# Four edits around softplus in a selective-scan kernel: where delta u is formed, how 1 - (1 + e) is added, which side steps stand beside the sums, when rows of B are fetched

## The chip, the core and the metric

The program runs on one core of a Trainium2 chip. Its time is the time of one execution on the device, in microseconds (us); of several runs the median is taken. Lower is better.

## The reference, cut to what matters

Four layers follow each other on an input of 8 images of 48 x 48 positions and 96 channels. Each layer normalises its input in groups of three channels, runs a two-dimensional selective scan on it, and adds the result to its input. The scan walks the 2,304 positions of an image in four orders (row by row and column by column, each forward and backward; K = 4), for 192 inner channels with 16 states each. Layers 0 to 2 have this form:

```python
xz = x @ in_proj_w.T
xpart, z = jnp.split(xz, 2, axis=-1)
xc = silu(depthwise_3x3(xpart) + conv_b)
xs = jnp.stack([x_hw, x_wh, x_hw[..., ::-1], x_wh[..., ::-1]], axis=1)   # four orders
x_dbl = jnp.einsum('bkdl,kcd->bkcl', xs, x_proj_w)
dts, Bs, Cs = jnp.split(x_dbl, [R, R + N], axis=2)
delta = jax.nn.softplus(jnp.einsum('bkrl,kdr->bkdl', dts, dt_proj_w) + dt_proj_b)
def step(h, inp):
    u_t, d_t, b_t, c_t = inp
    h = jnp.exp(d_t[..., None] * A) * h + (d_t * u_t)[..., None] * b_t[:, :, None, :]
    return h, jnp.einsum('bkdn,bkn->bkd', h, c_t)
```

The four outputs are turned back and added, with a skip term D u, then normalised over the channels, multiplied by silu(z) and projected back to 96 channels. Layer 3 computes the same scan by cumulative sums with a small term in a denominator; the kernel does it on the ends of the sequences alone and has a second run of the full sequences behind a condition at its end, which the profiled execution doesn't take.

What the change touches is delta = softplus(v) and the product delta u, which the scan reads as the factor of B.

## The kernel before, in words

**Tiling.** Work goes pair by pair of images (four pairs per layer). The 192 channels of two images make three tiles of 128 partitions: channels 0 to 127 of each image, and the last 64 of both together. For one pair there are 12 groups (tile t, phase ph for rows or columns, direction d), each of three chunks of 768 positions, each chunk of 16 units. A unit n carries two states: the 128 partitions hold 64 channels of state n // 2 and the same 64 channels of state n // 2 + 8, and n % 2 says which half of the channels it is. So layers 0 to 2 have 3 x 4 x 36 = 432 chunks and 6,912 units.

**One unit.** B is wanted as one row spread over 64 partitions, multiplied by delta u; da = exp(delta A); then comes the scan h = da h + b, then h C, then the sum over states.

- Units 2, 5, 7, 10, 13 and 15 are *pooled*: B comes by DMA in spread form (`bb`), POOL multiplies it by delta u (`weigh`, L741), ACT writes the exponential into a PSUM buffer named `b` (L764), DVE scans (L798).
- The other ten take B from rows in SBUF (`brow`) that PE spreads into the PSUM buffer `b` by a bf16 matmul (`spread_rows`, L667); DVE multiplies it by delta u (L794) and scans (L798); the exponential goes to SBUF (`da`, L764).
- In both, POOL multiplies h by the spread row of C (`cb`, L807), and PE adds the products of the states up in the PSUM buffer `acc` (`add_up`, L854), two units later. The two `b` buffers are shared by all units in turn, so unit n can fill its one only after the scan of unit n - 2.

**Softplus.** The generator `prepare` makes delta and delta u for one chunk while the 16 units of the chunk before it run; each `yield` is one step, and one step is taken per unit. A chunk has two halves of 384 positions. For a half: PE forms v (L603); ACT forms e = exp(-|v|), relu(v), then log(1 + e), w1 = 1 + e and w1 = 1 - w1 (L611 to L617); PE adds e + (1 - (1 + e)) + log(1 + e) + relu(v) into one PSUM bank by identity matmuls, in two steps (L623), where e + (1 - (1 + e)) is what the rounding of 1 + e lost; ACT copies the sum four times to SBUF, so that each half of the channels stands on both halves of the partitions (`to_twins`, L578, tile `dl`); DVE multiplies the bank by u in place (`times_u`, L631 for ph 0, L634 for ph 1); ACT copies that four times as well (L578, tile `du`). In layer 3 (class `Edge`, 192 positions) there is one copy and one product.

**Side steps.** The next pair's prologue (convolution, projections) and the last pair's epilogue (normalisation, gate, output projection) are generators too. In `beside`, one side step is taken per unit, none in unit 2; a step is for example one convolution matmul (L312), or an evacuation on ACT.

**Order.** Between two marks the kernel keeps every engine's instructions in the order in which the loop over units issues them. In unit n: the loads of units ahead (`load_b` 5 ahead, `load` 4 ahead), the spread of unit n + 1, the exponential of unit n + 3, the small carry copies on ACT (L682), the product and scan of unit n, the sum of unit n - 2, and `beside`. All DMAs go through SP's queue; the rows of B of a chunk (`brow`, two DMAs, L749) are issued together with the first `cb` of that chunk, in unit 12 of the chunk before.

Of the kernel before, what the change touches and what calls it, by code (L numbers as in the profile page):

```python
# [103 lines left out]
def ss2d_layers_kernel(ctx: ExitStack, tc: tile.TileContext, x_in, consts, weights, out):  # L104
# [55 lines left out]
    nc.vector.tensor_copy(pick, sel[: 2 * NR])  # L160


    twin = cpool.tile([P, 64], F32, name="twin")
    nc.vector.tensor_add(twin, ident[:, 0:64], ident[:, 64:P])

# [14 lines left out]
    nc.vector.tensor_add(centre, ident, off)  # L180
    centre_22 = cpool.tile([P, P], F32, name="centre_22")
    nc.vector.tensor_add(centre_22, ident, off_22)
    minus_group = cpool.tile([DM, DM], F32, name="minus_group")
    nc.scalar.activation(minus_group, group_w, AF.Copy, scale=-1.0)

# [96 lines left out]

    GATED, READY = "gated", "ready"

    def prologue(l, p, short=False, first=False):
        ly = layers[l]
# [282 lines left out]
                state[c.l, c.p]["xd"][c.ph, b, c.d * r : (c.d + 1) * r, c.c0 : c.c0 + c.m],  # L571
            )

    def to_twins(z, at, v):

        for g in range(2):
            for h in range(2):
                nc.scalar.copy(z[64 * h : 64 * h + 64, g, at], v[64 * g : 64 * g + 64])  # L578

    def prepare(c):  # L580
        l, p, t, ph, d = c.l, c.p, c.t, c.ph, c.d
        ly, s = layers[l], state[l, p]
# [10 lines left out]
        for z in range(0, c.m, HALF):  # L593
            m = min(HALF, c.m - z)
            at = slice(z, z + m)

            ps = bank()
            v = ps[:, :m]
            for b in c.batches:
                q0 = 32 * b if t == 2 else 0  # L600
                o = ps[64 * b : 64 * b + 64] if t == 2 else ps
                chans = slice(P, DIN) if t == 2 else slice(0, P)
                nc.tensor.matmul(  # L603
                    o[:, :m], ly.dtw[q0 : q0 + r, k, chans], dts[q0 : q0 + r, at],
                    start=True, stop=True,
                )
# [10 lines left out]
            nc.scalar.activation(w1, w1, AF.Identity, bias=ones, scale=-1.0)  # L617
            yield
            v = bank()[:, :m]
            for i, z1 in enumerate((e, w1, lg, x)):  # L620
                for g in range(2):
                    half = slice(64 * g, 64 * g + 64)
                    nc.tensor.matmul(  # L623
                        v[half], ident[:, half], z1, start=(i == 0), stop=(i == 3)
                    )
                if i % 2 == 1:
                    yield

            def times_u(o):
                if ph == 0:  # L630
                    nc.vector.tensor_mul(o, v, u[:, c.c0 + z : c.c0 + z + m])  # L631
                    return
                r0 = (c.c0 + z) // H
                nc.vector.tensor_mul(  # L634
                    o.rearrange("p (w h) -> p w h", h=H),
                    v.rearrange("p (w h) -> p w h", h=H),
                    u[:, r0 : r0 + m // H, :],
                )

            if isinstance(c, Edge):  # L640
                nc.scalar.copy(c.dl[0], v)
                times_u(c.du[0])
                c.sum_up()
                c.ready = True
                yield
                return

            to_twins(dl, at, v)
            if z + m == c.m:
                if l == NLAYER - 1:  # L650
                    c.sum_up()
                c.ready = True
                yield
            times_u(v)
            yield
            to_twins(du, at, v)
            yield


    def pieces(m):  # L660
# [23 lines left out]
    class Chunk:  # L684
# [52 lines left out]
        def weigh(self, n):  # L737

            if self.pooled(n):
                b = self.b[n][:, : self.m]  # L740
                nc.gpsimd.tensor_mul(b, b, self.du[n % 2])  # L741

        def load(self, n):

            s, m, at = state[self.l, self.p], self.m, slice(self.c0, self.c0 + self.m)
            if n == 0:
                self.brow = rpool.tile([2 * NR, SCAN], BF16, name="brow", tag="brow")
                for j, b in enumerate(range(2) if self.t == 2 else (self.t, self.t)):
                    nc.sync.dma_start(  # L749
                        self.brow[NR * j : NR * j + NR, :m],  # L750
                        s["xb"][self.ph, b, :, self.d, :, at],
                    )
            self.cb[n] = cb = cbpool.tile([P, SCAN], F32, name="cb", tag="cb")
            self.fetch(cb, NS, n)

# [414 lines left out]
    def run(pairs, short):  # L1170
# [58 lines left out]
        for k, ((l, p, unit), c, n) in enumerate(todo):  # L1229
# [172 lines left out]
```

## Time and profile before

| what | value |
|---|---|
| median of 3 runs | 20507.62 us (20500.42 to 20517.71) |
| the profiled execution: its time / its span | 20509.65 us / 20507.7 us |
| busy: POOL, DVE, PE, ACT | 17768.2, 17656.0, 17283.2, 16243.7 us |
| mean granted clock of TensorE | 0.904 |
| DMA, mean over the span | 205 GB/s |
| layers 0 to 2 (scans of L798), first and last | 205 us to 18,562 us |

In the profile a line of a group gives the source line, engine, operation, tiles, shapes and count, then the busy time in us and the mean of one instruction in ns, then the idle time of the engine just before these instructions and what ended most of it. A busy PE is not a PE at its peak, since matmuls are pipelined and their ends are modelled. An fp32 matmul appears as two records.

### The profile page before, as it was taken

The numbers are of one execution on the slowest core, as the hardware profiler recorded it, in microseconds if no ns is written. First come the engines' busy times: TensorE is split into PE (matmuls) and PEld (weight loads), VectorE is DVE, ScalarE is ACT, GpSimd is POOL, SyncE is SP. The second block draws the span as 40 slices with busy tenths as digits, with TensorE's granted clock in tenths as the row PEclk, the third lists the DMA queues.
The fourth block names the chain that finished last, engine by engine and source line by source line (L and its number), as shares of the span: only waits on it lengthen the run. The fifth ranks groups of instructions, "written<-read, shape, count | busy, mean of one in ns | idle before, by whom it ended". The sixth has DMA issues, their size and how long they took to land. (4 is left out here: it accounts for less than half of the span.)

```text
span 20507.7 us, 304889 instructions
## 1 busy us (share of the span) xinstructions
PE 17283.2 (84%) x88322; PEld 7546.6 (37%) x88322; DVE 17656.0 (86%) x14161; ACT 16243.7 (79%) x30020; POOL 17768.2 (87%) x10121
## 2 busy tenths in 40 slices
PE   8888888888888888888888888888888888888886
PEld 2323333333333333333333333333333333335565
DVE  5999999999999999999999999989989989995543
ACT  5777887887887887887877887877877877877776
POOL 5999999999999999999999999999999999995432
PEclk8998998998998999998998999988988998999997
DMA  5888888888888888888888888888888888883221
GB/s 147 223 221 222 219 220 224 222 219 221 220 225 222 219 229 221 221 229 219 221 228 220 217 225 219 218 218 220 217 219 219 220 219 222 219 220 109 76 72 51
DMA packets 1963444, 4200.13 MB, mean 205 GB/s; under 512 B 369456, under 2 KB 720048, under 8 KB 1948592
## 3 DMA queue, kind: packets, MB, share of 16 engines
q1 hardware_dynamic: 1961776, 4180.52, 77.8%
q8 instruction: 726, 11.89, 0.3%
q14 instruction: 942, 7.72, 0.2%
HBM read 4026.64 MB, written 152.27 MB: 204 GB/s over the span
## 5 line engine op out<-in xcount | busy, mean ns | idle before, releaser
L807 POOL TENSOR_TENSOR cb<-cb,da 128x768 f32<-128x768 f32 x4320 | 7831.3, 1817 | 799.5 <-issue 258.3
L854 PE MATMUL acc<-cb,twin 128*64 128x384 f32 x27648 | 7018.1, 542 | 663.6 <-POOL cb L807 660.3
L798 DVE TENSOR_TENSOR_SCAN da<-da,carry,b 128x768 f32<-128x768 f32 x2880 | 5223.3, 1814 | 176.4 <-ACT b L764 2.3
L741 POOL TENSOR_TENSOR bb<-bb,du 128x768 f32<-128x768 f32 x2592 | 4714.0, 1819 | 361.0 <-DMA bb<-xd 207.8
L794 DVE TENSOR_TENSOR b<-du,b 128x768 f32<-128x768 f32 x4320 | 4087.6, 946 | 883.9 <-PE b L667 785.4
L807 POOL TENSOR_TENSOR cb<-cb,bb 128x768 f32<-128x768 f32 x2592 | 4705.1, 1815 | 155.0 <-DVE bb L798 57.1
L667 PE MATMUL b<-brow,pick 96*64 96x512 bf16 (+2 forms) x18816 | 2761.6, 355 | 1787.6 <-DVE da L798 1408.4
L764 ACT ACTIVATE da<-dl,a 128x768 f32<-128x768 f32 x4320 | 4013.6, 931 | 245.8 <-POOL cb L807 214.0
L854 PEld LDWEIGHTS acc<-cb,twin 128*64 128x64 f32 x27648 | 2268.9, 150 | 3089.4 <-issue 1400.3
L798 DVE TENSOR_TENSOR_SCAN bb<-b,carry,bb 128x768 f32<-128x768 f32 x1728 | 3109.0, 1799 | 114.8 <-ACT b L764 53.5
L764 ACT ACTIVATE b<-dl,a 128x768 f32<-128x768 f32 x2592 | 2334.4, 901 | 590.2 <-DVE da L798 558.4
L798 DVE TENSOR_TENSOR_SCAN da<-da,b 128x768 f32<-128x768 f32 x1440 | 2525.4, 1754 | 85.6 <-DVE b L794 0.9
L667 PEld LDWEIGHTS <-pick 96*64 96x64 bf16 x18816 | 974.1, 114 | 4192.1 <-DVE da L798 2506.3
L578 ACT COPY dl<-ps 64x384 f32<-64x384 f32 x3456 | 1635.3, 473 | 756.7 <-PE ps L623 720.7
L312 PE MATMUL ps<-pad,diag 128*128 128x480 f32 (+1 forms) x4320 | 2165.7, 599 | 11.5 <-DVE eyc L1087 9.9
L623 PE MATMUL ps<-du,cst 128*64 128x384 f32 (+1 forms) x7296 | 1709.7, 516 | 93.1 <-ACT du L617 77.0
L578 ACT COPY du<-ps 64x384 f32<-64x384 f32 x3456 | 1635.7, 473 | 190.0 <-DVE ps L634 91.2
L798 DVE TENSOR_TENSOR_SCAN bb<-b,bb 128x768 f32<-128x768 f32 x864 | 1502.2, 1739 | 94.9 <-ACT b L764 40.5
L623 PE MATMUL ps<-dl,cst 128*64 128x384 f32 (+1 forms) x7296 | 1412.4, 483 | 0.0
L312 PEld LDWEIGHTS ps<-pad,diag 128*128 128x128 f32 x4320 | 687.5, 191 | 1211.4 <-issue 1090.1
L603 PE MATMUL ps<-dts,w 6*128 6x384 f32 (+5 forms) x2432 | 946.3, 595 | 176.1 <-DMA dts<-xd 103.7
L611 ACT ACTIVATE du<-ps,w 128x384 f32<-128x384 f32 (+1 forms) x912 | 521.4, 572 | 622.3 <-PE ps L603 611.5
(144 smaller groups left out, 19159.8 us busy)
## 6 DMA issues: line engine op xcount, KB each, us to landing
cb<-xd SPq DMA_DIRECT2D x13952, 192.0 KB
bb<-xd SPq DMA_DIRECT2D x5184, 192.0 KB
brow<-xb SPq DMA_DIRECT2D x864, 72.0 KB
yd<-y SPq DMA_DIRECT2D x48, 1152.0 KB
ey<-yd SPq DMA_DIRECT2D x256, 216.0 KB
cb<-xd SPq DMA_DIRECT2D x128, 384.0 KB
ex<-xs SPq DMA_DIRECT2D x256, 108.0 KB
xd<-xt SPq DMA_DIRECT2D x32, 684.0 KB
```

Source lines behind the costliest of these rows:

```text
L312: nc.tensor.matmul(ps[:, :m], ly.diag[:, int(t == 2), j, :], pad[:, r0 + dy : r0 + dy + nr, dx : dx + W], start=(j == 0), stop=(j == 8),)
L578: nc.scalar.copy(z[64 * h : 64 * h + 64, g, at], v[64 * g : 64 * g + 64])
L603: nc.tensor.matmul(o[:, :m], ly.dtw[q0 : q0 + r, k, chans], dts[q0 : q0 + r, at], start=True, stop=True,)
L611: nc.scalar.activation(e, v, AF.Abs, bias=bias)
L623: nc.tensor.matmul(v[half], ident[:, half], z1, start=(i == 0), stop=(i == 3))
L667: nc.tensor.matmul(o[64 * h : 64 * h + 64], pick[:, b, n : n + 1].to_broadcast([2 * NR, 64]), rows, start=True, stop=True,)
L741: nc.gpsimd.tensor_mul(b, b, self.du[n % 2])
L764: nc.scalar.activation(da, self.dl[n % 2], AF.Exp, scale=layers[self.l].a2[:, int(self.t == 2), n % 2, k, i : i + 1],)
L794: nc.vector.tensor_mul(b, self.du[n % 2], b)
L798: nc.vector.tensor_tensor_scan(way(h), way(da), way(b), start, ALU.mult, ALU.add)
L807: nc.gpsimd.tensor_mul(c, c, h)
L854: nc.tensor.matmul(self.acc[64 * g : 64 * g + 64, a, : self.m // 2], twin, c[:, a, :], start=False, stop=(pair + 2 == NS and not self.turns),)
```

## The change

1. **Delta u ahead of delta's copies, in SBUF.** `times_u` now writes `du[:, 0]` in SBUF and not the PSUM bank, and stands one step ahead of the four copies of delta. The twins of delta u are made by three copies from SBUF to SBUF, since the first of them is where DVE put it.
2. **1 - (1 + e) by a constant row.** ACT's second operation on w1 goes. PE starts each bank with a row of ones (two bf16 matmuls of `unit` with `unit_row`), subtracts w1 by a negated identity `less`, and then adds e, log and relu. The negated identity takes the place of a constant in `cst` that is not read later.
3. **Side steps.** The two steps of each half that issue sums yield `HEAVY`, and `beside` takes no side step there; in units 4, 12 and 14 it takes two.
4. **Rows of B.** `load_rows` issues a chunk's two `brow` DMAs in unit 6 of the chunk before it, in the same pair.

With the changed yields a chunk's steps fall otherwise on the units: the second half's sums on units 10 and 11 (9 and 10 before), its copies of delta on the top of unit 13 (unit 11 before), its copies of delta u on the end of unit 13 as before; the first half's sums stay on units 2 and 3, its copies of delta move from unit 4 to 5 and those of delta u from 5 to 6; the product with u stays on units 4 and 12.

```diff
+    less = cst[:, P : 2 * P]
+    unit = cpool.tile([P, 64], BF16, name="unit")
+    nc.gpsimd.memset(unit, 0.0)
+    nc.gpsimd.memset(unit[0:1], 1.0)
+    unit_row = cpool.tile([P, 1], BF16, name="unit_row")
+    nc.gpsimd.memset(unit_row, 1.0)
...
+    nc.scalar.activation(less, ident, AF.Copy, scale=-1.0)
...
             nc.scalar.activation(w1, e, AF.Identity, bias=ones)
-            nc.scalar.activation(w1, w1, AF.Identity, bias=ones, scale=-1.0)
             yield
             v = bank()[:, :m]
-            for i, z1 in enumerate((e, w1, lg, x)):
+            for g in range(2):
+                nc.tensor.matmul(
+                    v[64 * g : 64 * g + 64], unit, unit_row.to_broadcast([P, m]),
+                    start=True, stop=False,
+                )
+            for w, z1 in ((less, w1), (ident, e), (ident, lg), (ident, x)):
                 for g in range(2):
                     half = slice(64 * g, 64 * g + 64)
-                    nc.tensor.matmul(
-                        v[half], ident[:, half], z1, start=(i == 0), stop=(i == 3)
-                    )
-                if i % 2 == 1:
-                    yield
+                    nc.tensor.matmul(v[half], w[:, half], z1, start=False, stop=(z1 is x))
+                if z1 is e or z1 is x:
+                    yield HEAVY
...
-            to_twins(dl, at, v)
+            times_u(du[:, 0, at])
+            yield
+            for g in range(2):
+                for h in range(2):
+                    nc.scalar.copy(dl[64 * h : 64 * h + 64, g, at], v[64 * g : 64 * g + 64])
             if z + m == c.m:
                 if l == NLAYER - 1:
                     c.sum_up()
                 c.ready = True
+            yield
+            for h in (1, 0):
+                nc.scalar.copy(du[64 * h : 64 * h + 64, 1, at], du[64:P, 0, at])
+            nc.scalar.copy(du[64:P, 0, at], du[0:64, 0, at])
+            if z + m < c.m:
                 yield
-            times_u(v)
-            yield
-            to_twins(du, at, v)
-            yield
...
+            if n == 6 and coming_to < len(chunks):
+                z = chunks[coming_to]
+                if (z.l, z.p) == (l, p):
+                    z.load_rows()
...
             def beside():
-                step(coming)
-
-                for _ in range(10 if l in short else 0 if ends else 1):
+                got = next(coming, None)
+                some = 0 if ends or got is HEAVY else 2 if n in (4, 12, 14) else 1
+                for _ in range(10 if l in short else some):
                     side_step(rest) or side_step(behind, ahead)
```

`load_rows` holds the two `brow` DMAs that stood in `load`; `load` of a chunk's unit 0 calls it, and it does nothing where the rows are there already.

More of the change, by code (lines that the diff above doesn't have):

```diff
@@ L281, in ss2d_layers_kernel @@
     place = {"tiles": 3}
-    GATED, READY = "gated", "ready"
+    GATED, READY, HEAVY = "gated", "ready", "heavy"
     def prologue(l, p, short=False, first=False):
@@ L572, in load_dt @@
             )
[L574 to L578, printed above, removed]
     def prepare(c):
@@ L741, in weigh, with load_rows @@
                 nc.gpsimd.tensor_mul(b, b, self.du[n % 2])
+        def load_rows(self):
+            if self.brow is not None:
+                return
+            self.brow = rpool.tile([2 * NR, SCAN], BF16, name="brow", tag="brow")
+            for j, b in enumerate(range(2) if self.t == 2 else (self.t, self.t)):
+                nc.sync.dma_start(
+                    self.brow[NR * j : NR * j + NR, : self.m],
+                    state[self.l, self.p]["xb"][
+                        self.ph, b, :, self.d, :, self.c0 : self.c0 + self.m
+                    ],
+                )
         def load(self, n):
-            s, m, at = state[self.l, self.p], self.m, slice(self.c0, self.c0 + self.m)
             if n == 0:
[L747 to L752, printed above, removed]
+                self.load_rows()
             self.cb[n] = cb = cbpool.tile([P, SCAN], F32, name="cb", tag="cb")
```

## The prediction

> **What bounds the kernel now.** I read the busy times first, then the stretch of layers 0 to 2 alone, the groups by form, the waits, and a stretch of the timeline. The page's first part, and one window without the start and without layer 3:
>
> ```profile
> PE 17283.2 (84%) x88322; PEld 7546.6 (37%) x88322; DVE 17656.0 (86%) x14161; ACT 16243.7 (79%) x30020; POOL 17768.2 (87%) x10121
> ...
> 300.00:18560.00 18260.00, 15474.38 (x77729) 6322.09 (x77730) 16678.49 (x12545) 14660.40 (x27083) 16969.05 (x9632) 0.91 0.85 221
> ```
>
> In the window (its columns: us; busy PE, PEld, DVE, ACT, POOL; clock, DMA share, GB/s) POOL is busy 93% and DVE 91%. 432 chunks take 18,357 us (205 to 18,562), 42.5 us each; DVE works about 38.9 of them and POOL about 40. So no engine is full; what is lost is lost in waits between two nearly full engines. The groups by form (columns as in section 5 of the page):
>
> ```profile
> L807 POOL TENSOR_TENSOR cb<-cb,da 128x768 f32<-128x768 f32 x4320 | 7831.3, 1817 | 799.5 <-issue 258.3 <-DVE da L798 140.6 <-PE acc L854 66.0
> ...
> L741 POOL TENSOR_TENSOR bb<-bb,du 128x768 f32<-128x768 f32 x2592 | 4714.0, 1819 | 361.0 <-DMA bb<-xd 207.8 <-DMA cb<-xd 55.0 <-DVE da L798 25.5
> L807 POOL TENSOR_TENSOR cb<-cb,bb 128x768 f32<-128x768 f32 x2592 | 4705.1, 1815 | 155.0 <-DVE bb L798 57.1 <-issue 26.1 <-DMA cb<-xd 18.0
> L794 DVE TENSOR_TENSOR b<-du,b 128x768 f32<-128x768 f32 x4320 | 4087.6, 946 | 883.9 <-PE b L667 785.4 <-PE acc L854 89.7 <-PE ps L413 1.5
> ...
> L578 ACT COPY du<-ps 64x384 f32<-64x384 f32 x3456 | 1635.7, 473 | 190.0 <-DVE ps L634 91.2 <-DVE ps L631 52.8
> L578 ACT COPY dl<-ps 64x384 f32<-64x384 f32 x3456 | 1635.3, 473 | 756.7 <-PE ps L623 720.7
> ...
> L617 ACT ACTIVATE du<-du,ones 128x384 f32<-128x384 f32 x864 | 531.7, 615 | 28.2
> ...
> L634 DVE TENSOR_TENSOR ps<-ps,u 128x384 f32<-128x384 f32 x432 | 352.2, 815 | 126.0 <-ACT dl L578 116.3
> ...
> L631 DVE TENSOR_TENSOR ps<-ps,u 128x384 f32<-128x384 f32 x432 | 239.2, 554 | 207.7 <-ACT dl L578 196.3
> ```
>
> POOL loses 799.5 + 361.0 + 155.0 = 1,315.5 us, all that a change could win here. DVE loses 883.9 us before its products with B, almost all to PE's spread rows, and about 201 us (of 312.6; the rest is one wait of 104 us at the start and others outside the window) before the products with u, which wait for the copies of delta. Taking the 4,320 products of L794 in order, ten to a chunk, the idle time falls on units 0, 1 and 11 (83.7, 237.9, 304.2 us); the other seven have 258 together. Why unit 11, the timeline shows:
>
> ```profile
> 6085.33 0.54 PE L854 MATMUL acc<-cb,twin 128*64 128x384 f32 x1 [1.64 <-POOL cb L807]
> ...
> 6085.71 1.77 PE L623 MATMUL ps<-du,cst 128*64 128x384 f32 x7
> ...
> 6087.41 1.04 PE L465 MATMUL ps<-u,w 64*96 64x480 f32 x2
> ...
> 6088.38 0.52 PE L667 MATMUL b<-brow,pick 96*64 96x512 bf16 x4
> ...
> 6088.94 0.96 DVE L794 TENSOR_TENSOR b<-du,b 128x768 f32<-128x768 f32 x1 [1.49 <-PE b L667]
> ```
>
> PE's sum of an earlier unit waits for POOL, and then the softplus sums (1.77 us) and a side step (1.04 us, with about 0.6 us of issue ahead of it) stand before the spread rows of unit 11. Unit 10 is pooled, so DVE has only a scan to do meanwhile, and stalls.
>
> [...] L631 and L634 waited for L578. [...] PE waited 178.9 us in 50 places for rows of B here.
>
> **The change part by part**, per chunk (two halves) and times 432.
>
> *Spread rows of unit 11.* The sums now stand after them. I keep 35 us of the 304 (units 8 and 9 have 27 and 24): 269 us won. The next to stand behind sums are units 4 and 12. Unit 4 has it already, with 9 us of idle in all; unit 12 follows an unpooled unit and has 62.
>
> *Products with u.* They need PE's sums only, which ended a unit before. Their idle of 201 us goes: 190 won. Writing SBUF costs nothing: layer 3's products already do, 355 ns for 192 elements, which is on the same slope as 554 ns for 384.
>
> *Rows of B and the chunk's turn.* Units 0 and 1 lose 322 us, some of it the 178.9 us of rows. The two SP issues (about 0.75 us each) move from unit 12 to 6, past six units of `cb` and `bb` loads; they wait only for an older DMA, the buffer is long free. They get out of the way of the next chunk's first `cb` and `bb`. I take 190 us won; bounds 90 and 320.
>
> *ACT's operation and copies.* L617 goes: 864 x 0.615 = 532 us. Copies of delta u: 3,456 x 0.473 = 1,636 us become 2,592; [...] ACT works 0.85 ms less, but is busy 80% in the window, so this alone is worth nothing on the path; nor is the 720.7 us that it no longer waits for sums.
>
> *Constant rows.* 1,824 bf16 matmuls; a spread of 2 x 512 + 2 x 256 columns takes 0.52 us, so a pair of 384 some 0.25 us: 0.23 ms on PE, ahead of the spread of units 4 and 12. Those end 1.0 and 0.6 us before DVE takes them, so 0; without that cover 0.5 us per chunk, 216 us.
>
> *Side steps.* As many as before (15 of 16 units). Three leave units 3, 10 and 11, three come to 4, 12 and 14. PE idles 1.1 us before the spread of unit 14 and 1.8 us before that of the next unit 0, both for a scan; a second convolution step (1.07 + 0.6 us) fits. Zero.
>
> *The new wait.* In unit 13 ACT now has in a row: delta's four copies (first waiting for the product with u), the exponential of the next chunk, a carry, delta u's three copies, side work, and only then the exponential of unit 15, which DVE's scan of 15 waits for. Averaged over the chunks of the trace, from the end of scan 12: the product with u ends at 0.59, exponential 15 ran 3.03 to 3.93, scan 15 began at 5.17. ACT now starts copying at 0.62 (it follows DVE by 33 ns); + 4 x 0.485 = 2.56; + 0.84 = 3.40; + 0.1 to 0.2; [...] + 0.33 of side work (as now) = 5.2; + 0.90 = 6.1; + 0.09 = 6.2. Scan 15 is 1.0 us late: 430 us lost. If the second side step of unit 12 also waits for PE there, 2 us. Downward it is 0 only if POOL's lag (it takes unit 15 some 2.5 us after the scan) hides it. What is late next: scans 0 and 1; part of the wait for PE there is covered by it, counted above.
>
> *Layer 3 and start:* 48 x about 0.4 us of ACT less: 10 us at most.
>
> Sum: 269 + 190 + 190 - 430 + 10 = 229 us won. Against the profiled execution's 20,509.65 (span 20,507.7 and 2 us around it): 20,281. It is 2 us from the median of the runs, so the forecast is **20,280 us**.
>
> **Rivals.**
> - *The bunch on ACT is hidden, the gains come whole.* POOL, not DVE, sets the pace over a chunk's turn. For it: POOL's slack after scan 15. Against it: POOL waits 221 us before unit 1, so the slack is used up two units later. 269 + 190 + 190 less a quarter that POOL (40 of 42.5 us) can't follow: some 490 us, 20,010.
> - *Slower: the exponential of unit 15 falls further behind.* A step of the epilogue with table loads (1.28 us each), or an evacuation that waits for a matmul of the same unit, stands between delta's copies and it. The sign turns when the mean delay passes 649 / 432 = 1.5 us; at 2.0 us: 864 - 659 = 205 lost, 20,710.
> - *Nothing to measure.* Delay of 1.5 us, 20,507. Within 0.2% (41 us), about what a measurement of this kernel can tell from no change.
> - *The rows of B weren't late for their own sake* but behind large transfers, and `cb` and `bb` stay late: takes 100 to 190 us from the forecast; inside its range.
>
> **How the numbers follow.** Forecast case 0.46, own range 20,130 to 20,440 (delay 0.65 to 1.35 us); gains whole 0.20; nothing 0.13; slower 0.21. Faster 0.66, within 0.2% 0.13, slower 0.21. The range leaves about one in ten on each side: half of the whole-gain case and half of the slower one, 19,970 to 20,690.
>
> **What would show it.** Idle before L794's successor at unit 11 near 30 us, not 304. No wait of the products with u on ACT; ACT's copies of delta wait for DVE. PE's waits on rows of B gone. A new wait of the pooled scans for ACT's `b`, 94 us in the window now, of 300 to 500 us, all at unit 15: if it is under 150, the gains come whole; over 650, it is slower. POOL's idle near 1,090 us. Wrong in kind: if PE's spread rows at units 12, 14 or 0 take the place of unit 11, or POOL's instructions lengthen from 1.82 us.

## The result, and the profile after

The changed kernel takes 20,750.57 us (median of 4 runs, 20,730.57 to 20,767.26) against 20,512.67 us for the kernel before on the same chip. The ratio is 1.0113, with a 95% interval of 1.0096 to 1.0131: 238 us slower, where 229 us faster was forecast, and above the upper end of the range (20,690). The profiled execution took 20,767.26 us (span 20,765.5).

The first line below is the busy time of the engines on the page of the changed kernel; the second is the window of layers 0 to 2, without the start and without layer 3 (us; busy PE, PEld, DVE, ACT, POOL; clock, DMA share, GB/s).

```profile
PE 17439.9 (84%) x90146; PEld 7598.8 (37%) x90146; DVE 17633.7 (85%) x14161; ACT 15409.7 (74%) x28247; POOL 17777.8 (86%) x10124
...
300.00:18800.00 18500.00, 15614.07 (x79376) 6357.82 (x79372) 16629.28 (x12527) 13836.58 (x25351) 16957.97 (x9621) 0.91 0.86 218
```

POOL is as busy as before (17,777.8 us against 17,768.2) and DVE too; ACT has 834 us less to do. The time is therefore in waits. TensorE's granted clock was 0.905, before 0.904, and so doesn't account for the loss. POOL's share of the window fell from 93% to 92%, DVE's from 91% to 90%. The groups by form of the changed kernel (busy us, mean ns, then the idle time just before them and its releasers):

```profile
L822 POOL TENSOR_TENSOR cb<-cb,da 128x768 f32<-128x768 f32 x4320 | 7844.3, 1819 | 1056.3 <-DVE da L813 398.6 <-issue 274.3 <-DMA cb<-xd 78.3
...
L749 POOL TENSOR_TENSOR bb<-bb,du 128x768 f32<-128x768 f32 x2592 | 4715.2, 1819 | 378.6 <-DMA bb<-xd 176.1 <-DMA cb<-xd 91.0 <-ACT carry L690 21.9
L822 POOL TENSOR_TENSOR cb<-cb,bb 128x768 f32<-128x768 f32 x2592 | 4713.2, 1818 | 128.6 <-issue 78.3 <-DVE bb L813 18.9 <-DMA cb<-xd 16.8
L809 DVE TENSOR_TENSOR b<-du,b 128x768 f32<-128x768 f32 x4320 | 4080.6, 945 | 679.7 <-PE b L675 665.4 <-ACT du L663 5.4 <-PE ps L420 4.7
...
L813 DVE TENSOR_TENSOR_SCAN bb<-b,carry,bb 128x768 f32<-128x768 f32 x1728 | 3117.3, 1804 | 468.5 <-ACT b L779 372.8 <-DMA cb<-xd 39.3 <-POOL bb L749 17.2
...
L655 ACT COPY dl<-ps 64x384 f32<-64x384 f32 x3456 | 1638.4, 474 | 997.3 <-DVE du L637 534.1 <-DVE du L634 426.7
...
L662 ACT COPY du<-du 64x384 f32<-64x384 f32 x1728 | 881.7, 510 | 25.5
```

The products with B (L809) wait 679.7 us against 883.9, the products with u no longer wait for ACT, and the copies of delta wait for DVE instead. POOL, however, is idle 1,563.5 us in these three groups against 1,315.5, and the increase is nearly all "DVE da L813": POOL waits for scans that come late. The waits of DVE in the same window say why (engine, line, what it waited for: us in total, times, longest us):

```profile
DVE b L809 <- PE b L675: 657.6, 506, 5.2
DVE bb L813 <- ACT b L779: 526.1, 434, 4.2
DVE eyc L1102 <- ACT ps L277: 111.3, 43, 4.3
DVE eyc L1080 <- ACT ps L1078: 100.2, 45, 3.3
```

Before, the second was 94.1 us in 66 places, and the epilogue's two products of `eyc` waited 14 us together. Two kinds of waiting have been added to DVE. The first was forecast: the scan of unit 15 waits for ACT's exponential. One case, in a stretch of the timeline of the changed kernel:

```profile
7492.91 0.53 DVE L634 TENSOR_TENSOR du<-ps,u 128x384 f32<-128x384 f32 x1
...
7493.48 1.95 ACT L655 COPY dl<-ps 64x384 f32<-64x384 f32 x4 [2.15 <-DVE du L634]
...
7495.45 0.94 ACT L779 ACTIVATE da<-dl,a 128x768 f32<-128x768 f32 x1
...
7496.48 1.03 ACT L662 COPY du<-du 64x384 f32<-64x384 f32 x2
...
7497.55 0.51 ACT L663 COPY du<-du 64x384 f32<-64x384 f32 x1
7497.97 0.90 ACT L779 ACTIVATE b<-dl,a 128x768 f32<-128x768 f32 x1
...
7498.95 1.82 DVE L813 TENSOR_TENSOR_SCAN bb<-b,carry,bb 128x768 f32<-128x768 f32 x1 [1.07 <-ACT b L779]
```

ACT works without a gap through four copies of delta, the next chunk's exponential, three copies of delta u, and only then writes the exponential that the scan wants; the scan is 1.07 us late. The second kind was not forecast. Another stretch of the same trace, in unit 14:

```profile
7050.61 0.90 ACT L779 ACTIVATE b<-dl,a 128x768 f32<-128x768 f32 x1
...
7051.53 0.94 ACT L779 ACTIVATE da<-dl,a 128x768 f32<-128x768 f32 x1
...
7052.57 0.59 ACT L1077 ACTIVATE ps<-ps,ln_eps 128x432 f32<-128x432 f32 x1
...
7053.20 0.52 ACT L1078 ACTIVATE ps<-ps 128x432 f32<-128x432 f32 x1
...
7053.74 0.60 DVE L1080 TENSOR_TENSOR eyc<-eyc,ps 128x432 f32<-128x432 f32 x1 [3.34 <-ACT ps L1078]
...
7054.27 1.75 DVE L813 TENSOR_TENSOR_SCAN bb<-b,bb 128x768 f32<-128x768 f32 x1
```

Here `beside` took two side steps: ACT's logarithm and exponential of the epilogue, and the DVE product that reads them. The exponential for the scan of unit 15 was there at 7051.51; the scan starts at 7054.27, because the product L1080 stands ahead of it in DVE's queue and waits 3.34 us for ACT, which came to it late.

The idle time by unit follows from the same trace when the 432 chunks' instructions are taken in order (us, first to last scan of layers 0 to 2, which took 18,356.6 us before and 18,616.2 after):

| idle time of | before | after |
|---|---|---|
| DVE before products with B: units 0, 1, 11 / the other seven | 84, 238, 304 / 258 | 42, 190, 56 / 391 |
| of these, unit 9 | 24 | 118 |
| DVE before products with u | 226 | 2 |
| DVE before scans of units 15, 7, 2 | 37, 47, 11 | 467, 146, 41 |
| DVE before the two products of `eyc` | 14 | 212 |
| DVE in all | 1,595 | 1,882 |
| POOL before products with C: units 0 and 1 | 233 | 517 |
| POOL before products with C: units 5 and 14 | 288 | 98 |
| POOL before products with C: unit 11 | 81 | 14 |
| POOL before products with C: units 9 and 15 | 91 | 284 |
| POOL in all | 1,302 | 1,553 |

The stretch became 260 us longer, DVE's idle time 287 us and POOL's 251 us. The two sums alone prove nothing: both engines have the same work in both kernels, so their idle time must grow with the stretch. What points to a cause is where it lies. Of the 212 us before the products of `eyc`, 153 lie in unit 14, which is one of the doubled units and stands behind ACT's bunch in unit 13.

### The profile page after: what moved, and what is told of

It is laid out like the page before. It is cut to its first block, busy times and chain, and to the rows that moved or that the text cites. A ratio compares the mean times of both kernels' runs of the same rounds, so it can differ in the third digit from the quotient of the medians.

```text
span 20765.5 us, 307668 instructions
## 1 busy us (share of the span) xinstructions
PE 17439.9 (84%) x90146; PEld 7598.8 (37%) x90146; DVE 17633.7 (85%) x14161; ACT 15409.7 (74%) x28247; POOL 17777.8 (86%) x10124
## 4 chain that ended last, share of the span: by engine, by line
PE 29%; DVE 18%; ACT 18%; DMA 18%; issue 12%; SPq 3%; POOL 2%; DVEq 0%; POOLq 0%; ACTq 0%
DVE da L813 9%; DMA cb<-xd 8%; PE acc L869 7%; DMA bb<-xd 7%; DVE b L809 5%; PE ps L628 5%; PE ps L319 4%; ACT b L779 4%; PE b L675 3%; ACT da L779 3%; ACT dl L655 3%; PE acc L854 2%; DVE bb L813 2%; SPq L732 2%; POOL cb L822 2%
## 5 line engine op out<-in xcount | busy, mean ns | idle before, releaser
L869 PE MATMUL acc<-cb,twin 128*64 128x384 f32 x27648 | 6908.2, 538 | 543.2 <-POOL cb L822 532.9
L813 DVE TENSOR_TENSOR_SCAN da<-da,carry,b 128x768 f32<-128x768 f32 x2880 | 5223.0, 1814 | 177.9 <-ACT b L779 3.2
L809 DVE TENSOR_TENSOR b<-du,b 128x768 f32<-128x768 f32 x4320 | 4080.6, 945 | 679.7 <-PE b L675 665.4
L675 PE MATMUL b<-brow,pick 96*64 96x256 bf16 (+2 forms) x18816 | 2619.4, 354 | 1679.4 <-DVE da L813 1445.3
L813 DVE TENSOR_TENSOR_SCAN bb<-b,carry,bb 128x768 f32<-128x768 f32 x1728 | 3117.3, 1804 | 468.5 <-ACT b L779 372.8
L813 DVE TENSOR_TENSOR_SCAN da<-da,b 128x768 f32<-128x768 f32 x1440 | 2525.4, 1754 | 87.3 <-ACT b L779 1.4
L675 PEld LDWEIGHTS <-pick 96*64 96x64 bf16 x18816 | 879.1, 114 | 4177.5 <-DVE da L813 2647.8
L655 ACT COPY dl<-ps 64x384 f32<-64x384 f32 x3456 | 1638.4, 474 | 997.3 <-DVE du L637 534.1
L319 PE MATMUL ps<-pad,diag 128*128 128x480 f32 (+1 forms) x4320 | 2073.9, 589 | 40.3 <-DVE eyc L1080 26.8
L813 DVE TENSOR_TENSOR_SCAN bb<-b,bb 128x768 f32<-128x768 f32 x864 | 1505.4, 1742 | 259.5 <-ACT b L779 155.5
L628 PE MATMUL ps<-du,cst 128*64 128x384 f32 (+1 forms) x7296 | 1463.9, 518 | 107.0 <-ACT du L617 105.3
L628 PE MATMUL ps<-dl,cst 128*64 128x384 f32 (+1 forms) x7296 | 1343.5, 482 | 0.0
L662 ACT COPY du<-du 64x384 f32<-64x384 f32 x1728 | 881.7, 510 | 25.5
```

The costliest lines, as they stand in the source:

```text
L319: nc.tensor.matmul(ps[:, :m], ly.diag[:, int(t == 2), j, :], pad[:, r0 + dy : r0 + dy + nr, dx : dx + W], start=(j == 0), stop=(j == 8),)
L628: nc.tensor.matmul(v[half], w[:, half], z1, start=False, stop=(z1 is x))
L655: nc.scalar.copy(dl[64 * h : 64 * h + 64, g, at], v[64 * g : 64 * g + 64])
L662: nc.scalar.copy(du[64 * h : 64 * h + 64, 1, at], du[64:P, 0, at])
L675: nc.tensor.matmul(o[64 * h : 64 * h + 64], pick[:, b, n : n + 1].to_broadcast([2 * NR, 64]), rows, start=True, stop=True,)
L809: nc.vector.tensor_mul(b, self.du[n % 2], b)
```

## The experiments

The theory after the result: two costs add up. One is the forecast bunch on ACT in unit 13: the four copies of delta and three of delta u, behind which the exponential for the scan of unit 15 comes late. The other is the doubled side steps, which put an ACT step and the DVE step that reads it into one unit. The rivals: the bunch alone is the cause, at a larger price than forecast; or the parts are each harmless and only their meeting costs. The first three kernels undo one or both of the suspects in the changed kernel; the next four make each part alone in the kernel before; the last four join parts or move one. Times in brackets are those of the kernel before in the same batch. Waits of an experiment are those of the window 300 to 18,560 us, which holds layers 0 to 2 but for a last piece in the slower kernels; idle times by unit are of all 432 chunks.

**Copies of delta u one unit later.** In the changed kernel one more step is taken before the second half's copies of delta u, so they go out in unit 14, behind the exponential of unit 15.

```diff
                 c.ready = True
+                yield
             yield
             for h in (1, 0):
```

> The changed kernel with one edit: the three copies of delta u of a chunk's second half go out in unit 14, behind the exponential of unit 15, and not in unit 13. Theory A (ACT's bunch in unit 13 makes the scan of unit 15 late): DVE's waits for ACT's exponentials into b fall from 528 us to under 170 us, the idle before the scan of unit 15 from 467 us to under 100 us, and the time falls by 280 to 400 us, to 20,350 to 20,470 us. Theory B (the doubled side steps and PE cause the loss, the bunch only takes up slack that something else would take): the wait goes, but the time stays over 20,650 us, with the idle time moved to DVE's products with B of units 0 and 1.

Measured: 20,597.07 us (20,509.81), ratio 1.0047 (1.003 to 1.0064), some 154 us below the changed kernel. The waits of DVE:

```profile
DVE b L810 <- PE b L676: 762.7, 565, 5.8
DVE bb L814 <- ACT b L780: 206.7, 182, 3.5
DVE eyc L1103 <- ACT ps L277: 105.0, 50, 4.7
DVE b L810 <- ACT du L664: 97.6, 212, 0.8
DVE eyc L1081 <- ACT ps L1079: 91.3, 36, 3.2
```

The wait for the exponential falls from 526 to 207 us, and the scan of unit 15 from 467 to 84. So the copies of delta u are what made it late. But the time falls by less than half of that, and by less than the 280 to 400 us of theory A: the idle time before the products of units 0 and 1 grew from 232 to 425 us. Half of this growth has the edit itself as its source. The late copies are now waited for: the fourth line, 98 us, is the product of unit 0 waiting for delta u. So the 154 us are what the bunch costs less what its cure costs. The epilogue's products wait as before, and the kernel is still slower than the kernel before: the bunch alone is not the cause.

**One side step per unit.** The changed kernel with `beside` as it was before.

```diff
-                got = next(coming, None)
-                some = 0 if ends or got is HEAVY else 2 if n in (4, 12, 14) else 1
-                for _ in range(10 if l in short else some):
+                step(coming)
+
+                for _ in range(10 if l in short else 0 if ends else 1):
```

> The changed kernel with the side steps of the kernel before: one in every unit but unit 2, sums or not. Theory B: a doubled side step puts ACT's part of the epilogue and the DVE product that reads it into one unit, so the 212 us that DVE waits before the epilogue's two products in layers 0 to 2 fall to under 40 us; the time falls by 100 to 200 us, to 20,550 to 20,650 us. Theory A alone: those waits aren't on the path, the sums get a side step beside them again, and the time stays within 60 us of 20,750 us or rises. In both the scan of unit 15 still waits for ACT, some 400 us.

Measured: 20,582.69 us, ratio 1.0037 (1.0023 to 1.0051), 168 us below the changed kernel. The waits of DVE:

```profile
DVE b L809 <- PE b L675: 649.6, 548, 4.8
DVE bb L813 <- ACT b L779: 410.7, 369, 5.4
...
DVE eyc L1102 <- ACT ps L277: 50.4, 40, 2.1
...
DVE eyc L1080 <- ACT ps L1078: 43.7, 39, 1.5
```

The epilogue's products wait 95 us instead of 212, and the scan of unit 7 is back at 20 us (146 in the changed kernel). 95 is more than was expected: with one step per unit ACT still comes late to the epilogue's work while it has the bunch to do (61 of the 95 us lie in unit 14; in the next kernel, without the bunch, 5 us). The wait for the bunch itself is there (scan of unit 15: 508 us).

**Both.** The two edits above together.

> Both edits: copies of delta u of the second half in unit 14, side steps as before. If the two causes are separate and both on the path, their gains add: 20,150 to 20,300 us, faster than the kernel before by 1 to 1.7 percent. If they hide each other, less than the larger of the two alone plus 60 us. If PE behind sums and side steps takes over, over 20,450 us, with the idle before DVE's product of unit 12 over 200 us.

Measured: 20,360.94 us, ratio 0.9925 (0.9908 to 0.9941). The two suspects together are worth 390 us. That is more than the sum of the two alone (154 + 168 = 322), but by the intervals such a difference of two kernels is good to some 50 us only. Without them the change is faster than the kernel before. The scan of unit 15 waits 115 us, the products of `eyc` 42. The gain is less than had been expected (20,150 to 20,300): units 0 and 1 keep 388 us of idle time. In this kernel TensorE's granted clock was 0.917, and PE's sums over states took 533 ns where they took 542 before; whether this is a part of the gain or follows from it, no run separates. The last three kernels below have a higher clock too (0.911 to 0.917).

**Rows of B alone.** The kernel before with only `load_rows` and its call in unit 6.

```diff
             if n == 0:
-                self.brow = rpool.tile([2 * NR, SCAN], BF16, name="brow", tag="brow")
-                for j, b in enumerate(range(2) if self.t == 2 else (self.t, self.t)):
-                    nc.sync.dma_start(
...
+                self.load_rows()
...
+            if n == 6 and coming_to < len(chunks):
+                z = chunks[coming_to]
+                if (z.l, z.p) == (l, p):
+                    z.load_rows()
```

> The kernel before with one part of the change: rows of B fetched in unit 6. The prediction took 190 us (90 to 320) for it: 20,320 to 20,420 us, PE's 179 us of waits for rows gone and the idle before DVE's products of units 0 and 1 down from 322 to some 130 us. The rival: the rows were late behind other transfers, whose lateness stays, so that cb and bb are waited for instead: within 40 us of 20,510 us.

Measured: 20,460.93 us (20,509.81), ratio 0.9978 (0.9971 to 0.9985): 49 us faster. PE's wait for rows of B, 176.8 us in 48 places before, is gone. The idle time of unit 0 falls from 84 to 11 us, that of unit 1 rises from 238 to 256. POOL's groups by form show what was given back (before: 361.0 idle, of it 207.8 for `bb` and 55.0 for `cb`):

```profile
L741 POOL TENSOR_TENSOR bb<-bb,du 128x768 f32<-128x768 f32 x2592 | 4719.6, 1821 | 351.2 <-DMA bb<-xd 188.9 <-DMA cb<-xd 100.1 <-ACT du L578 16.7
```

The idle time before POOL's products with B has not gone, it has moved: in unit 2 it falls from 184 to 44 us, in units 13 and 15 it rises from 73 to 212. All loads are issued on SP's queue, where an issue for rows of B takes 749 ns (median in the kernel before), and behind the two put in at unit 6 the `bb` come later: from its issue to its use the `bb` of unit 15 has 7.8 us, where it had 8.5.

**Products with u alone.** Delta u in SBUF and the products ahead of the copies, in the kernel before, with its own ACT operation, its own side steps and rows.

```diff
-            to_twins(dl, at, v)
+            times_u(du[:, 0, at])
+            yield
+            for g in range(2):
+                for h in range(2):
+                    nc.scalar.copy(dl[64 * h : 64 * h + 64, g, at], v[64 * g : 64 * g + 64])
...
-                yield
-            times_u(v)
-            yield
-            to_twins(du, at, v)
             yield
+            for h in (1, 0):
+                nc.scalar.copy(du[64 * h : 64 * h + 64, 1, at], du[64:P, 0, at])
+            nc.scalar.copy(du[64:P, 0, at], du[0:64, 0, at])
+            if z + m < c.m:
+                yield
```

> The kernel before with the first part alone: product with u ahead of delta's copies, into SBUF, three copies of delta u, and the yields that go with it. Theory A (this part brings the bunch on ACT): no wait of the products with u, the idle before DVE's product of unit 11 under 90 us (304 before), but 430 to 530 us before the scan of unit 15 (37 before) and over 90 us before the product of unit 9 (24 before); in time a loss of 90 to 150 us, 20,600 to 20,660 us. If the bunch comes from the parts together, the scan of unit 15 waits under 200 us and the kernel is faster than before.

Measured: 20,563.17 us (20,507.63), ratio 1.0027 (1.0016 to 1.0038): 56 us slower.

```profile
DVE b L799 <- PE b L672: 628.8, 505, 6.2
DVE bb L803 <- ACT b L769: 426.2, 375, 5.4
```

Unit 11's stall falls from 304 to 94 us and the products with u wait 3 us. The scan of unit 15 waits 491 us. So this part alone, with both stalls cured as forecast, loses. POOL's idle time by unit says how: 81 to 35 us at unit 11, 288 to 91 at units 5 and 14, but 233 to 454 at units 0 and 1 and 6 to 35 at unit 15.

**The constant row alone.** PE's row of ones and the negated identity, without ACT's second operation on w1, in the kernel before.

```diff
-            nc.scalar.activation(w1, w1, AF.Identity, bias=ones, scale=-1.0)
...
-            for i, z1 in enumerate((e, w1, lg, x)):
+            for g in range(2):
+                nc.tensor.matmul(
+                    v[64 * g : 64 * g + 64], unit, unit_row.to_broadcast([P, m]),
+                    start=True, stop=False,
+                )
+            for w, z1 in ((less, w1), (ident, e), (ident, lg), (ident, x)):
```

> The kernel before with the second part alone: the constant row and the negated identity on TensorE, one ACT operation less per half. The prediction took it for nothing on the path: 20,470 to 20,550 us, ACT 530 us less busy. The rival: the sums stand in front of the spread rows of unit 11 and wait there for ACT's chain, which is one operation shorter now, so the idle before the product of unit 11 falls from 304 to some 200 us and the time to 20,400 to 20,460 us.

Measured: 20,572.62 us (20,507.63), ratio 1.0033 (1.0021 to 1.0046): 65 us slower. DVE's wait for PE's spread rows (779.9 us before):

```profile
DVE b L803 <- PE b L676: 967.2, 850, 5.3
```

ACT works 516 us less, and nothing comes of it. PE has two more matmuls per half ahead of the spread rows (110 us more busy time), and unit 11 goes from 304 to 360 us of idle time, unit 6 from 83 to 111. The reading is that those rows came late in the kernel before already, so that what is put ahead of them is paid.

**The side steps alone.** `HEAVY` and the doubled units, in the kernel before.

```diff
                 if i % 2 == 1:
-                    yield
+                    yield HEAVY
...
-                step(coming)
-
-                for _ in range(10 if l in short else 0 if ends else 1):
+                got = next(coming, None)
+                some = 0 if ends or got is HEAVY else 2 if n in (4, 12, 14) else 1
+                for _ in range(10 if l in short else some):
```

> The kernel before with the third part alone: no side step beside the sums (here units 2, 3, 9 and 10), two in units 4, 12 and 14. Theory B: DVE waits 150 to 220 us before the epilogue's two products in layers 0 to 2 (14 before), and some 150 us are won before the product of unit 11, so it ends between 20,500 and 20,620 us. The prediction's own reading (moved side steps cost nothing, the spread rows of unit 11 come sooner): 20,280 to 20,400 us.

Measured: 20,501.2 us (20,507.63), ratio 0.9998 (0.999 to 1.0007): no difference. The waits of DVE:

```profile
DVE b L794 <- PE b L667: 588.1, 526, 5.0
DVE bb L798 <- ACT b L764: 232.5, 157, 3.9
...
DVE eyc L1087 <- ACT ps L270: 83.8, 91, 2.5
```

This is a gain and a loss that cancel. Without a side step beside the sums, unit 11 falls from 304 to 131 us and the products with u from 226 to 112. The doubled units cost about as much: 91 us more at `eyc`, 94 at the scan of unit 7, 60 at that of unit 2, 51 and 56 at the products of units 0 and 14.

**The products and the side steps together.** This is the test of the meeting of parts: alone they make +56 and -6 us, so 50 if they add. To the kernel with the products alone come the edits just shown:

```diff
-                    yield
+                    yield HEAVY
...
-                for _ in range(10 if l in short else 0 if ends else 1):
+                got = next(coming, None)
+                some = 0 if ends or got is HEAVY else 2 if n in (4, 12, 14) else 1
+                for _ in range(10 if l in short else some):
```

> The kernel before with the first and the third part together (products ahead of the copies with their yields; no side step beside the sums, two in units 4, 12 and 14), without constant row and rows ahead. Alone they cost 56 us and gain 6 us. Theory C (both relieve the same stalls, at unit 11 and before the products with u, so together they gain that once and pay both prices: the scan of unit 15 waits for ACT, and DVE waits for ACT's part of the epilogue and at unit 7): 20,700 to 20,760 us, DVE's waits before the epilogue's products about 200 us, before the scan of unit 15 over 400 us. If the extra loss of the whole change comes from the constant row beside doubled side steps, or from the rows, the two together add up: 20,540 to 20,600 us.

Measured: 20,740.72 us (20,492.25), ratio 1.0121 (1.0104 to 1.0138): 248 us slower, not 50.

```profile
DVE b L799 <- PE b L672: 629.2, 484, 5.3
DVE bb L803 <- ACT b L769: 510.9, 435, 4.2
DVE eyc L1092 <- ACT ps L270: 103.7, 36, 4.3
DVE eyc L1070 <- ACT ps L1068: 99.9, 44, 3.3
```

In DVE's idle time against the kernel before (us):

| | products alone | side steps alone | sum | together |
|---|---|---|---|---|
| before products with B | -232 | -191 | -424 | -233 |
| before products with u | -223 | -114 | -337 | -223 |
| before scans | +432 | +178 | +610 | +519 |
| before `eyc` | +97 | +91 | +188 | +191 |
| in all | +70 | -36 | +34 | +251 |

(What the rows lack of the last one, at most 4 us, lies before other work.) Both parts cure the same two stalls, so together the cure counts once, and both prices are paid. The changed kernel does the same: it differs from this one only by the constant row and the rows of B.

**Both suspects undone, rows in unit 3.** The third kernel, with the call of `load_rows` three units earlier (layers 0 to 2).

```diff
-            if n == 6 and coming_to < len(chunks):
+            if n == 3 and l not in short and coming_to < len(chunks):
```

> The third of the runs so far (copies of delta u in unit 14, one side step in each unit) with rows of B fetched in unit 3 and not in unit 6. If the two DMAs in unit 6 hold up the bb of units 13 and 15, which POOL then waits 153 and 146 us for (20 and 53 in the kernel before), they now go before the bb of unit 10, which has the longest lead (9.4 us from issue to use): the waits of 13 and 15 fall under 80 us each and the time by 40 to 100 us, to 20,260 to 20,320 us. If two more DMAs cost the same wherever they stand, it stays within 30 us of 20,361 us and the wait shows at unit 10.

Measured: 20,320.22 us (20,507.63), ratio 0.9908 (0.9891 to 0.9924), 41 us below the third kernel by the medians; the intervals overlap. POOL's idle time before its products with B falls from 298 to 109 us at units 13 and 15 (25 and 84) and appears at unit 10 (87 to 187): it moved again, and less came back than went.

**The products, with late copies of delta u.** The kernel before with the products' part and the late copies; no constant row, no doubled steps, rows as before. Against the kernel with the products alone:

```diff
                 c.ready = True
+                yield
             yield
```

> The kernel before with the first part alone, and the copies of delta u of a chunk's second half in unit 14. With the whole change but the side steps this edit gained 222 us. If it does the same here: 20,563 less 222, 20,320 to 20,370 us, the idle before the scan of unit 15 under 130 us (491 without the edit), and the first part alone is then faster than the kernel before by 0.7 to 0.9 percent. If the gain hung on the shorter ACT chain of the constant row, it is under 100 us here, over 20,460 us.

Measured: 20,354.28 us (20,492.25), ratio 0.9934 (0.9917 to 0.995). Against the products alone this is 207 us less idle time of POOL (1,137 against 1,344) and 1.0027 against 0.9934 in the ratio, some 190 us: that is the net price of the bunch on ACT for the program, while DVE's idle time before the scan of unit 15 differs by 420 us (491 to 71). It is a net price because the late copies have one too. Two of DVE's waits and one of POOL's in this kernel:

```profile
DVE bb L804 <- ACT b L770: 139.0, 125, 3.8
DVE b L800 <- ACT du L661: 100.3, 219, 0.7
...
POOL bb L747 <- ACT du L661: 78.4, 69, 4.4
```

The last two are waits for the copies of delta u at the chunk's turn, before the product of unit 0 and before POOL's `bb` of unit 2. With the products alone DVE has no such wait in this window, and POOL a single one of 17 us.

**The same with the rows of B in unit 3.** To this comes `load_rows`, called from unit 0 as in the change and ahead of it here:

```diff
+            if n == 3 and l not in short and coming_to < len(chunks):
+                z = chunks[coming_to]
+                if (z.l, z.p) == (l, p):
+                    z.load_rows()
```

> The same with rows of B fetched in unit 3: the version that the runs so far point to, without the constant row (65 us lost alone) and without doubled side steps. If the parts add: 20,320 (both edits, rows in unit 3, with the constant row) less 65, 20,220 to 20,290 us. If the constant row pays beside the other parts, since it shortens ACT by 530 us, it is 20,320 us or more.

Measured: 20,269.2 us (20,492.25), ratio 0.9896 (0.9879 to 0.9912): 1.0% faster than the kernel before, and the fastest of all. The waits of DVE:

```profile
DVE b L807 <- PE b L673: 642.0, 545, 5.5
DVE bb L811 <- ACT b L777: 112.0, 115, 3.8
```

The rows are worth 85 us here, 49 in the kernel before. The two are not alike: here they go out in unit 3, there in unit 6, and this move alone made 41 us in the medians of the kernels with both suspects undone. This kernel differs from that one (rows in unit 3, 0.9908) by the constant row alone, and the ratios' intervals overlap: beside the other parts too, no gain of the constant row shows.

## Why the prediction was wrong

The signs that the prediction named for DVE, ACT and PE came (unit 11, the products with u, the rows, a new wait at unit 15), and PE's rows at units 12, 14 and 0 did not take unit 11's place. The new wait was larger than named, 526 us against 300 to 500, and not all at unit 15: the scan of unit 7 waits 146. The sign that failed outright is POOL's idle time: 1,563.5 us, where about 1,090 was named. So what was wrong is not what each stall would do, but what it is worth, and a cost that was put at nothing.

**Unit 11, "269 us won".** The stall went as said: 304 to 56 us, against 35. As a gain for the program it was mis-sized. POOL had been idle for 81 us at unit 11, of which 67 were won. The two go together over the kernels: DVE's stall of 360, 304, 131, 94 and 56 us there (constant row, before, side steps, products, the whole change) stands beside 95, 81, 30, 35 and 14 us of POOL's. That POOL bridges the rest with pooled work in hand is the likely reason, not a shown one.

**Products with u, "190 won".** 226 to 2 us, and POOL's idle time at units 5 and 14, which follow those products, fell by 190. The mechanism held, and the size as far as POOL's idle time at these two units tells. Writing SBUF cost nothing, as said (533 and 786 ns where it took 554 and 815 in the bank). In the trace of the changed kernel no copy of delta overlaps a product with u: the first one starts 33 ns behind it at the earliest, and the copies now wait for DVE (961 us in the group L655). Whether the two could run at once, no run here shows.

**Both gains together, 269 + 190 = 459.** No run gives them whole. The products with late copies of delta u come nearest, since the scan of unit 15 waits only 71 us there, and that kernel is 138 us faster. DVE's idle time fell by 451 us at unit 11 and before the products with u, but rose by 88 at units 0 and 1 (where the late copies are waited for), 88 at unit 9 and 82 at unit 6. A stall that is cured at one place was in large part waited out at the next. This also speaks against the first rival, which took the gains whole.

**The new wait, "430 us lost".** At DVE it is right almost to the number: the scan of unit 15 went from 37 to 467 us. The length of delta u's three copies in its sum was the author's estimate, which no trace of the kernel before shows; in the case at 7,492 us they take 1.03 us for two and 0.51 for the third. For the program, taking it away is worth 154 us in the changed kernel, some 190 to 210 beside the products alone and 222 with one side step per unit (each good to some 50 us). POOL's lag may hide a part, as the prediction itself allowed; another part is that the late copies bring 100 us and 78 us of waits themselves. How the rest divides is open. "269 + 190 - 430", 29 us won, was measured as 56 us lost by the products alone. That this is so near is luck: the gains were taken some 320 us too high and the loss some 220 to 240 us too high. Among other items, the matmul that forms v for the new half (the dt matmul, L603) stands one unit later, and the product of unit 9 waits 118 us (before 24) behind it and the side step that follows it, in every kernel with the products' steps (112 to 132) and not in those without (22 to 34). This was not seen in the working.

**Side steps, "Zero".** This is the step that failed most: a cost put at nothing. It asked where PE has room for a second step, and PE has it by and large: the spread rows of units 12 and 14 stall DVE for 36 us (before 62) and 37 us (before 0). It did not ask which steps of which engine would be side by side. A step of ACT and the next one of DVE in the same unit make DVE wait for an ACT that is late itself, and the scan behind that step waits with it, since the kernel keeps each engine's order (3.34 us in the case at 7,050 us). In the changed kernel the doubled steps cost 168 us of program time, beside the late copies 236 (20,597 against 20,361); their own gain (unit 11 and the products with u) had already been counted under those two headings. The slower rival came near in number (20,710) and named the step (one of the epilogue with table loads, 1,283 ns each in the trace), but it let ACT's exponential fall further behind, and put the turn at 1.5 us of mean delay. That the number came near is luck. The scan of unit 15 was 1.0 us later, as in the forecast; the additional loss lies at `eyc` and at the scan of unit 7.

**Rows of B, "190 won".** 49 us alone, below the lower bound of 90. PE's waits for the rows are gone as said. But unit 1 doesn't wait for rows; and "past six units of `cb` and `bb` loads" was not priced for the loads that are delayed. For the DMAs that were moved the earlier issue was enough: PE no longer waits for them (176.8 us before). The loads behind them paid for it: in units 13 and 15 POOL waited 139 us more.

**Constant rows, "0".** 65 us lost. The step looked at units 4 and 12, where the rows end ahead of need, while the matmuls also stand ahead of other spread rows that are late: units 11 and 6.

**ACT's operation and copies, "worth nothing on the path".** Right as far as the runs tell: no kernel with less work on ACT shows a gain from it, but in each of them something else changed as well. The 0.85 ms took a length for the copies from SBUF to SBUF that no trace of the kernel before shows. Measured, such a copy took 510 ns (L662) and one from PSUM 474 (L655), and ACT's busy time fell by 834 us.

**Layer 3 and the start, 10.** The part behind the last scan of layer 2 went from 1,946.2 to 1,944.6 us.

The difference between forecast (229 won) and result (238 lost) is 467 us. By the measured kernels it divides so: side steps 165 (238 lost less the 73 lost with one step per unit), rows of B 141 (190 - 49), the products' three items 85 (29 + 56), the constant row 65, layer 3 about 8: 464. Three separate parts add up within what can be told: 56 + 65 - 49 = 72 against a measured 73 (interval 47 to 105). Only the side steps and the products do not. No single one of these differences turns the sign: with the side steps' 165 put right the forecast would still have been 64 us faster, and only with the rows' 141 as well does it become slower.

## What to carry to other kernels

When two engines near saturation take turns, do not book a stall's length as a gain. Look unit by unit at the idle time of the engine that comes after: here 304 us of DVE's stall at unit 11 stood beside 81 us of POOL's, while curing 226 us before the products with u took 190 us from POOL's. Even that is not the gain of the program: 451 us of cured stalls were worth 138 us, while new waits came elsewhere. Where two parts of a change cure the same stall, do not add their gains before a run shows the two together: here +56 and -6 us alone became +248, since both prices were paid and the cure counted once. A step that is put into a slot brings its engine's queue with it: ask not only whether the slot's busiest engine has room, but whether the next step, on another engine that keeps the program's order, reads what this one writes (here DVE's wait before the products of `eyc` went from 14 to 212 us).

## What was unexpected

Giving an engine less to do made nothing faster here (ACT, 516 to 834 us less), and a DMA moved earlier made others late: twice, at unit 6 (units 13 and 15, 73 to 212 us) and at unit 3 (unit 10, 87 to 187 us), the wait moved to the transfers queued behind it. The late exponential's price at DVE (some 420 us) and what the program gains without it (154 to 222 us) differ by a factor of two or more. What the doubled steps cost by engine order alone, with ACT not busy with the bunch, was only seen in sum (91 us at `eyc`, in the kernel with the side steps alone); which pairs of steps make it was not tried. Nor was it tried whether the dt matmul of the new half, put one unit back, would give the 94 us of unit 9.
